# Attention steps: queries and keys transposed by VectorE blocks and a DRAM round trip instead of TensorE, with each step's order written out by hand

## Chip, cores and metric

The kernel runs on one core of a Trainium2 chip. The metric is device microseconds of one launch. The kernel before took 1660.21 us, the median of three runs (1654.62 to 1660.83). Everything is float32.

## The reference

Four layers are added one after the other to x, eight sequences (batches) of 128 tokens by 512. Each layer is a conditioning block followed by a feed-forward block with low-rank experts. The change touches the conditioning block of the third layer (L2), which is an attention with a paged cache of keys and values:

```python
q = _rope(_rmsnorm(q, q_norm_w), pos); k = _rope(_rmsnorm(k, k_norm_w), pos)
kc = k_cache[block_table].reshape(bsz, L, HK, D)
k_all = jnp.concatenate([kc, k], axis=1); v_all = jnp.concatenate([vc, v], axis=1)
scores = jnp.einsum('bqhd,bkhd->bhqk', q, k_all) * SCALE
scores = jnp.where(valid[:, None, None, :], scores, -1e+30)
o = jnp.einsum('bhqk,bkhd->bqhd', jax.nn.softmax(scores, axis=-1), v_all)
return jnp.einsum('bse,de->bsd', o.reshape(bsz, seqlen, HQ * D), Wo)
```

There are 32 query heads and 8 key heads of 128 elements, so four query heads share a key head. Each batch has 512 cached keys, on 16 pages of 32, and 128 new ones. A score is a sum over the 128 head elements, so queries and keys must both lie with the head element on the partitions before the score matmul. Rope and the norm are made with the token on the partitions. Between the two lies a transpose, and that is what the change moves.

## The kernel before, in words

The span has three parts. The first two layers take about the first 320 us. The attention then runs as a loop in `run` (L1176) over 32 steps. The second half of L2 and the fourth layer (`ending`) follow from about 1454 us.

A step n is a pair (qd, p): one key head qd, with its four query heads, and one pair p of batches. For a given step the loop does these things.

- `weigh(n, j)` (L1053), for the pair's batches j = 0 and 1: five score matmuls of 128x512, one for each chunk of 128 keys, into PSUM tiles "st" (three buffers). ScalarE takes the exponential of each into pT.
- `added` (L1067): VectorE adds the five chunks of pT. `divisors` (L1075) sums them over the keys with four small matmuls, takes the reciprocal on VectorE, makes four copies of 32 partitions, and spreads them with three DMAs on SP into R.
- `mix(n, j)` (L1095): five matmuls with the values, accumulated in PSUM tile "av". VectorE multiplies the result by R.
- `project(n+1)` (L946) makes the next step's queries, key and value with `seven` (L908), a product in seven block products instead of eight. Its products one, six and five go through "mm" tiles, of which there are three. Its outputs c11, c12, c21 and c22 leave PSUM through ScalarE (c11) and VectorE (the other three, L961).
- `leave(n-1)` (L1112) is the same `seven` with the output weights. VectorE adds its four results to y2 (L1122), and GpSimd adds two more terms (L1125 and L1130).
- `rotate(n+1)` (L979) and `normed(n+1)` (L1012): GpSimd multiplies the halves of queries and key by the sine table (L990, tiles vq and vk); VectorE multiplies by the cosine table (L994), adds the two (L1018), and multiplies by the reciprocal root of the mean square (L1022), which ScalarE and one VectorE reciprocal prepare.
- `turn_cached(n+1)` (L1025) and `turn(n+1)` (L1036): 8 TensorE transposes of the gathered cached keys, two of the new keys and 8 of the queries, each with a matmul against the identity into PSUM. VectorE copies the keys out (L1033, L1042), and ScalarE the queries (L1049).
- `tokens` (L903) makes the four sums and differences of x that `seven` needs, on VectorE.
- `gather(n+1, "v")` and `gather(n+2, "k")` (L876): GpSimd issues eight indirect DMAs for the values of the next step and eight for the keys of the one after (L886). The gathered keys have two buffers, one for each batch of a pair.

[...] The function `kept` (L840) pins an instruction to its place in program order among the pinned ones of its engine. In the loop it covers GpSimd, most of VectorE and ScalarE, and the R transfers on SP. The matmuls, the PSUM evacuations and the weight loads are not pinned; a scheduler at compile time places them. GpSimd's order in a step is therefore fixed: vq and vk of step n+1, the two additions to y2, eight gathers of values, eight gathers of keys. The gathered keys of step n+1 are first read by `turn_cached(n+1)`, near the end of step n, after `mix(n, 0)` (L1206 to L1208).

Of the kernel before, what the change touches and what calls it, by code (L numbers as in the profile page):

```python
# [17 lines left out]
P = 128  # L18
# [29 lines left out]
def forward(ctx: ExitStack, tc: tile.TileContext, a: dict, out: bass.AP):  # L48
# [16 lines left out]
    rp = ctx.enter_context(tc.tile_pool(name="rp", bufs=1))  # L65
# [24 lines left out]
    second = gate_weights(1)  # L90

# [42 lines left out]
    def rows(name, n, where=const):  # L134
# [38 lines left out]
    selp = w0.tile([P, NB * 4, 4], F32, tag="selp", name="selp")  # L173
    dve.tensor_tensor(
        selp,
        table.rearrange("p (c j) -> p c j", j=4),
        block32.unsqueeze(1).to_broadcast([P, NB * 4, 4]),
        ALU.mult,
    )
    page = const.tile([P, NB * 4], F32, tag="page", name="page")  # L180
    dve.tensor_reduce(page, selp, AX.X, ALU.add)
    dve.tensor_scalar(page, page, 32.0, p_mod32, ALU.mult, ALU.add)
    kvrow = const.tile([P, NQ, NB * 4], I32, tag="kvrow", name="kvrow")
    for qd in range(NQ):
        dve.tensor_scalar(kvrow[:, qd, :], page, float(NQ), float(qd), ALU.mult, ALU.add)
# [472 lines left out]
    with psa:  # L658
# [11 lines left out]
        att = attention(tc, a, x, ident, lens, kvrow, part, ww, wop, ypool, sums, rot, ps_, c2, chunks, mm)  # L670
# [81 lines left out]
    with tc.If(redo > 0):  # L752
        sp.dma_start(x, kept)
        y2 = attention_any(tc, a, x, ident, lens, kvrow, part, ww, wop, ypool, rot, rows, chunks, mm)
# [23 lines left out]
def attention(tc, a, x, ident, lens, kvrow, part, ww, wop, ypool, sums, rot, psa, c2, chunks, mm):  # L778
# [12 lines left out]
    trig, straight, crossed, eps = rot  # L791
# [41 lines left out]
    S = {n: {} for n in range(len(steps))}  # L833
    W, WO = {}, {}
# [41 lines left out]
    def gather(n, what):  # L876
        qd, p = steps[n]
        t = []
        for j in range(2):
# [4 lines left out]
            for c in range(4):  # L884
                i = (2 * p + j) * 4 + c
                kept(pool.indirect_dma_start(  # L886
                    out=d[:, c, :], out_offset=None, in_=kc if what == "k" else vc,
                    in_offset=bass.IndirectOffsetOnAxis(ap=kvrow[:, qd, i : i + 1], axis=0),
                ))
# [12 lines left out]

    def tokens(n):  # L903
        b = 2 * steps[n][1]
        parts = [x[:, 2 * h : 2 * h + 2, (b + j) * P : (b + j + 1) * P] for j in range(2) for h in range(2)]
        S[n]["A"] = combine(wk.tile([P, 4, 2, P], F32, tag="xs", name=f"xs_{n}", bufs=1), *parts)

    def seven(A, B, name, u, two, out2, out4, c11, c12, c21, c22, between=lambda: None):  # L908
# [6 lines left out]

        def into(o, l, r, start):
            for c in range(2):
                pe.matmul(  # L918
                    o, l[:, c, :], r[:, c, :], start=start and c == 0, stop=c == 1, skip_group_check=True
                )  # L920
# [5 lines left out]
        act.copy(u[:, 0], one)  # L926
        into(p6, s2, t2, True)
        into(p5, s1, t1, fresh)
        dve.tensor_tensor(u[:, 1], p6, u[:, 0], ALU.add)
        dve.tensor_tensor(u[:, 2], p5, u[:, 1], ALU.add)  # L930
        into(six, s3, t3, True)
        c22(six, u[:, 2])
        between()
        into(one, a12, b21, False)
        c11(one)
        into(p5, s4, b22, False)
        c12(p5, u[:, 1])
        into(six, a22, t4, False)
# [7 lines left out]
    def project(n):  # L946
# [11 lines left out]
        def put(j, i):  # L958
            def f(ps, u):
                for to, at in places(j, i):  # L960
                    dve.tensor_tensor(to, ps[:, at], u[:, at], ALU.add)  # L961
            return f

        def copied(ps):
            for to, at in places(0, 0):
                act.copy(to, ps[:, at])  # L966

        def two():
# [6 lines left out]
            copied, put(0, 1), put(1, 0), put(1, 1),  # L975
        )
        S[n].update(q=q, k=k)

    def rotate(n):  # L979

        ssq = wk.tile([P, 2, REP + 1], F32, tag="ssq", name=f"ssq_{n}")

        def crossed_terms(m, t, nh):
# [3 lines left out]
            r = wk.tile(full, F32, tag="r" + m, name=f"r{m}_{n}", bufs=1)  # L987
# [9 lines left out]
        def squares(m, t, nh, at):  # L997
            for j in range(2):
                for i in range(nh):
# [988 lines left out]
```

## Time and profile before

| what | value |
|---|---|
| runs of the kernel before, median (lowest to highest) | 1660.21 us (1654.62 to 1660.83) |
| the profiled execution's own time | 1623.05 us |
| its span, first to last instruction | 1621.3 us |
| TensorE / VectorE / ScalarE / GpSimd busy | 1592.8 / 1066.4 / 564.5 / 825.6 us |
| from 457 to 1310 us (24 steps): TensorE / VectorE / ScalarE / GpSimd | 851.55 / 651.36 / 379.85 / 565.41 of 853.0 us |
| from 1454 us to the end: TensorE busy | 154.90 of 167.0 us |
| DMA over the span | 94.41 MB, mean 58 GB/s |
| DMA in the first 41 us | busy share 0.89, 301 GB/s |
| granted TensorE clock, mean | 0.994 |

PE is TensorE's matmuls, PEld its weight loads, DVE is VectorE, ACT ScalarE, POOL GpSimd and SP SyncE; an ending q means the engine's own queue of instructions that are not counted as busy. A profile line names the source line, the engine, the operation, output<-inputs, the shape and the count. A float32 matmul shows as two records. Matmuls overlap, so the pace of TensorE is read from the distance between starts, not from the duration of one record. Issuing a gather is an instruction on POOL (DMA_INDIRECT); its data land later.

### The profile page before, as it was taken

Reading aid. Unit: us, or ns where it says so; the run is one execution under the profiler, and the core shown is the slowest. Engines: PE = TensorE matmul, PEld = TensorE weight load, DVE = VectorE, ACT = ScalarE, POOL = GpSimd, SP = SyncE. Lnnn points to the kernel's source line nnn. Section 1 sums busy time; section 2 is a strip of 40 time slices with the busy share of each in tenths; the row PEclk is TensorE's granted clock in tenths of the full one; section 3 lists DMA queues with packets and bytes.
Section 4 is the critical chain, followed back from the end, with each engine's and each line's share of the span. In section 5 each row is a group of like instructions: output and inputs, shape, how many; then the busy total and the mean of one; then the engine's idle time right before and its main releaser. Section 6 shows DMA issues by size and latency. Waiting matters only on the chain.

```text
span 1621.3 us, 19398 instructions
## 1 busy us (share of the span) xinstructions
PE 1592.8 (98%) x6561; PEld 985.8 (61%) x6561; DVE 1066.4 (66%) x2224; ACT 564.5 (35%) x1390; POOL 825.6 (51%) x778
## 2 busy tenths in 40 slices
PE   9999999999999999999999999999999999999998
PEld 7878885445555555555555556555555655568653
DVE  4575524676878777687877868787786778753141
ACT  1111110254543444455344445544444554420210
POOL 2241106456666666666666656666665676710000
PEclk9999999999999999999999999999999999999899
DMA  8110002221111212112121212212121221311000
GB/s 304 34 39 24 1 1 72 73 61 56 56 64 43 85 43 73 52 61 64 41 87 41 74 48 66 62 43 85 43 73 46 68 62 40 95 49 47 0 18 37
DMA packets 69194, 94.41 MB, mean 58 GB/s; under 512 B 16800, under 2 KB 40544, under 8 KB 68960
## 3 DMA queue, kind: packets, MB, share of 16 engines
q1 hardware_dynamic: 50944, 56.09, 10.9%
q0 software_dynamic: 17056, 36.49, 7.7%
q8 instruction: 54, 0.88, 0.2%
q10 hardware_dynamic: 1088, 0.52, 0.1%
q14 instruction: 52, 0.43, 0.1%
HBM read 76.14 MB, written 4.33 MB: 50 GB/s over the span
## 4 chain that ended last, share of the span: by engine, by line
PE 87%; DVE 8%; issue 3%; POOL 2%; ACT 0%; DMA 0%; SPq 0%; ACTq 0%; DVEq 0%; POOLq 0%
PE av L53 15%; PE st L53 14%; PE q_six L918 7%; PE g L356 7%; PE q_one L918 5%; PE q_five L918 5%; PE wo_two L918 5%; PE dn L356 4%; PE wo_one L918 3%; PE wo_six L918 3%; PE eo_l L53 2%; PE z L53 2%; PE h L1557 2%; PE o L53 2%; DVE q_s L858 2%
## 5 line engine op out<-in xcount | busy, mean ns | idle before, releaser
L886 POOL DMA_INDIRECT kn<-in_k_cache,kvrow x256 | 276.5, 1080 | 80.2 <-issue 66.0
L886 POOL DMA_INDIRECT vals<-in_v_cache,kvrow x256 | 270.0, 1055 | 73.3 <-issue 38.9
L53 PE MATMUL av<-pT,vals 128*128 128x512 f32 x640 | 303.6, 597 | 0.0
L53 PE MATMUL st<-qT,kT 128*128 128x512 f32 x640 | 291.7, 593 | 0.0
L53 PEld LDWEIGHTS av<-pT,vals 128*128 128x128 f32 x640 | 116.5, 190 | 128.9 <-issue 128.9
L53 PEld LDWEIGHTS st<-qT,kT 128*128 128x128 f32 x640 | 116.7, 190 | 124.6 <-issue 96.9
L1061 ACT ACTIVATE pT<-st,hide 128x512 f32<-128x512 f32 x256 | 169.3, 686 | 37.5 <-PE st L53 34.7
L990 POOL TENSOR_TENSOR vq<-q,txq 128x512 f32<-128x512 f32 x64 | 83.5, 1326 | 152.8 <-DVE q L961 152.8
L1072 DVE TENSOR_TENSOR part<-pT 128x512 f32<-128x512 f32 x128 | 85.2, 689 | 64.7 <-ACT pT L1061 64.6
L1049 ACT COPY qT<-qTp 128x512 f32<-128x512 f32 x64 | 37.5, 586 | 206.2 <-PE qTp L1047 206.2
L1130 POOL TENSOR_TENSOR y<-y,uo 128x512 f32<-128x512 f32 x32 | 44.1, 1379 | 112.9 <-DVE y L1122 112.9
L918 PE MATMUL q_one<-q,x 128*128 128x384 f32 x256 | 96.2, 498 | 0.0
L918 PE MATMUL q_six<-q_s,xs 128*128 128x384 f32 x256 | 95.7, 492 | 0.0
L1001 ACT ACTIVATE sqq<-q 128x128 f32<-128x128 f32 x256 | 79.4, 310 | 8.3 <-DVE q L961 1.5
L918 PEld LDWEIGHTS q_six<-q_s,xs 128*128 128x128 f32 x256 | 49.1, 192 | 36.7 <-issue 4.8
L1018 DVE TENSOR_TENSOR rq<-rq,vq 128x1024 f32<-128x1024 f32 x32 | 70.3, 2198 | 1.2 <-POOL vq L990 1.2
L918 PE MATMUL wo_one<-o,oT 128*128 128x256 f32 x256 | 65.8, 379 | 0.0
L918 PEld LDWEIGHTS q_one<-q,x 128*128 128x128 f32 x256 | 46.0, 189 | 31.4 <-issue 6.0
L966 ACT COPY q<-q_one 128x256 f32<-128x256 f32 x32 | 11.9, 372 | 148.2 <-PE q_one L918 138.7
L1087 DVE RECIPROCAL r<-sum 128x128 f32<-128x128 f32 x64 | 60.7, 949 | 0.9 <-PE sum L1081 0.6
L1089 DVE COPY R<-r 32x128 f32<-32x128 f32 x256 | 58.9, 230 | 3.6
L918 PE MATMUL wo_two<-o_s,os 128*128 128x256 f32 x256 | 60.5, 379 | 0.0
(387 smaller groups left out, 2846.0 us busy)
## 6 DMA issues: line engine op xcount, KB each, us to landing
R<-R SPq DMA_DIRECT2D x192, 64.0 KB
q<-in_WqT SPq DMA_DIRECT2D x8, 1024.0 KB
o<-in_WoT SPq DMA_DIRECT2D x8, 1024.0 KB
kn<-in_k_cache,kvrow POOLq DMA_INDIRECT x256, 2.7
vals<-in_v_cache,kvrow POOLq DMA_INDIRECT x256, 2.6
wd<-in_WdT SPq DMA_DIRECT2D x2, 1280.0 KB
wg<-in_WgT SPq DMA_DIRECT2D x9, 256.0 KB
wu<-in_WuT SPq DMA_DIRECT2D x9, 256.0 KB
```

The source lines that it names most:

```text
L53: pe.matmul(o, lhsT, rhs, start=start, stop=stop)
L356: pe.matmul(o, lhsT, rhs, start=start, stop=stop, skip_group_check=True)
L886: kept(pool.indirect_dma_start(out=d[:, c, :], out_offset=None, in_=kc if what == "k" else vc, in_offset=bass.IndirectOffsetOnAxis(ap=kvro ...
L918: pe.matmul(o, l[:, c, :], r[:, c, :], start=start and c == 0, stop=c == 1, skip_group_check=True)
L990: kept(pool.tensor_tensor(u[:, :, :, lo : lo + 64], t[:, :, :, hi : hi + 64], wx[:, :, lo : lo + 64].unsqueeze(2).to_broadcast(part_), ALU ...
L1001: kept(act.activation(sq, t[:, j, i, :], AF.Square, accum_out=ssq[:, j, at + i : at + i + 1]))
L1018: kept(dve.tensor_tensor(r, r, u, ALU.add))
L1061: act.activation(pT[:, c, :, :].rearrange("p i t -> p (i t)"), ps, AF.Exp, bias=hide[:, b, c : c + 1] if c < 4 else 0.0,)
L1072: kept(dve.tensor_tensor(o, l, r, ALU.add))
L1087: kept(dve.reciprocal(r, ps))
L1089: kept(dve.tensor_copy(R[0:32, i * P : (i + 1) * P], r[32 * i : 32 * i + 32, :]))
L1130: kept(pool.tensor_tensor(t, t, u.unsqueeze(1).to_broadcast([P, 2, HW]), ALU.add))
```

## The change

Eighteen TensorE transposes a step go. In their place VectorE transposes blocks of 32x32, and two transfers through DRAM put the blocks in place: four writes on SP, one for each group of 32 partitions, and then a read back (one for the cached keys; one for the queries and two for the new keys). The pages of a gathered key tile are permuted (`kvrow["k"]`), so that the blocks come out in the order of the values.

- `turn_cached(n+1)` moves from the end of step n into the middle of `project(n+1)`, behind its c22.
- `turn(n+1)` moves into `leave(n-1)`, behind its c22, and its transposed queries have one buffer. The read into it waits until `weigh(n, 1)` has read the old ones.
- `rotate(n+1)` moves from the middle of `leave(n-1)` to its beginning.
- The new key is no longer multiplied by its reciprocal root; the factor goes into the scale of the fifth exponential.
- All matmuls, evacuations and transfers of a step are pinned. `mix(n, 0)` runs among and after the scores of `weigh(n, 1)`, `mix(n, 1)` closes step n, and the sums over the keys move into `project` behind its second product.
- The sums of `tokens` are kept from the first use on for the heads 1 to 6.

The diff, cut to its core:

```diff
+    kvrow = {}
+    for what, order in (("v", "p (b c j) -> p b c j"), ("k", "p (b j c) -> p b c j")):
+        selp = w0.tile([P, NB, 4, 4], F32, tag="selp", name="selp_" + what)
+        dve.tensor_tensor(
+            selp,
+            table.rearrange(order, b=NB, c=4),
+            block32.unsqueeze(1).unsqueeze(1).to_broadcast([P, NB, 4, 4]),
+            ALU.mult,
+        )
+        page = const.tile([P, NB * 4], F32, tag="page", name="page_" + what)
...
+    turned, turned_new = (
+        nc.dram_tensor("turned_" + name, (len(steps), 4, 32, 4, m, 32), F32, kind="Internal").ap()
+        for name, m in (("cached", 8), ("new", 2 * REP + 2))
+    )
...
+    kept_sums = {}
+
     def tokens(n):
-        b = 2 * steps[n][1]
+
+
+        qd, p = steps[n]
+        b = 2 * p
+        if 0 < qd < NQ - 1 and p in kept_sums:
+            S[n]["A"] = kept_sums[p]
+            return
         parts = [x[:, 2 * h : 2 * h + 2, (b + j) * P : (b + j + 1) * P] for j in range(2) for h in range(2)]
-        S[n]["A"] = combine(wk.tile([P, 4, 2, P], F32, tag="xs", name=f"xs_{n}", bufs=1), *parts)
-
-    def seven(A, B, name, u, two, out2, out4, c11, c12, c21, c22, between=lambda: None):
+        if 0 < qd < NQ - 1:
+            if not kept_sums:
+                late.append(late[0].tile([P, NP, 4, 2, P], F32, tag="yT", name="xs_all"))
+            S[n]["A"] = kept_sums[p] = combine(late[1][:, p], *parts)
+        else:
+            S[n]["A"] = combine(wk.tile([P, 4, 2, P], F32, tag="xs", name=f"xs_{n}", bufs=1), *parts)
...
+        def now(where):
+            if where in at:
+                at[where]()
...
-        act.copy(u[:, 0], one)
+        kept(act.copy(u[:, 0], one))
+        now("one")
         into(p6, s2, t2, True)
+        now("six")
         into(p5, s1, t1, fresh)
-        dve.tensor_tensor(u[:, 1], p6, u[:, 0], ALU.add)
-        dve.tensor_tensor(u[:, 2], p5, u[:, 1], ALU.add)
+        kept(dve.tensor_tensor(u[:, 1], p6, u[:, 0], ALU.add))
+        now("u1")
+        kept(dve.tensor_tensor(u[:, 2], p5, u[:, 1], ALU.add))
+        now("u2")
         into(six, s3, t3, True)
         c22(six, u[:, 2])
-        between()
+        now("c22")
         into(one, a12, b21, False)
         c11(one)
+        now("c11")
         into(p5, s4, b22, False)
         c12(p5, u[:, 1])
+        now("c12")
...
+        both = wk.tile([P, 2 * REP + 2, HD], F32, tag="r", name=f"r_{n}", bufs=1)
+        views = {"q": both[:, 0 : 2 * REP], "k": both[:, 2 * REP :]}
...
+    def rotated(n):
+        for m in "qk":
+            r, u = S[n]["r" + m]
+            kept(dve.tensor_tensor(r, r, u, ALU.add))
+
+    def roots(n):
+        s = S[n]
+        s["rs"] = rs = wk.tile([P, 2, REP + 1], F32, tag="rs", name=f"rs_{n}")
+        kept(act.activation(rs, s["ssq"], AF.Sqrt, bias=eps, scale=1.0 / HD))
 
     def normed(n):
+
         s = S[n]
-        s["rest"]()
-        rs = wk.tile([P, 2, REP + 1], F32, tag="rs", name=f"rs_{n}")
-        kept(act.activation(rs, s["ssq"], AF.Sqrt, bias=eps, scale=1.0 / HD))
-        for r, u in (s["rk"], s["rq"]):
-            kept(dve.tensor_tensor(r, r, u, ALU.add))
+        r, rs = s["rq"][0], s["rs"]
         kept(dve.reciprocal(rs, rs))
-        for m, at, nh in (("k", REP, 1), ("q", 0, REP)):
-            r = s["r" + m][0]
-            dve.tensor_tensor(r, r, rs[:, :, at : at + nh].unsqueeze(3).to_broadcast([P, 2, nh, HD]), ALU.mult)
-            s[m] = r
+        kept(dve.tensor_tensor(r, r, rs[:, :, 0:REP].unsqueeze(3).to_broadcast([P, 2, REP, HD]), ALU.mult))
...
     def turn_cached(n):
 
         s = S[n]
-        kT = wk.tile([P, 2, LK], F32, tag="kT", name=f"kT_{n}")
+        t = wk.tile([P, 4, 8, 32], F32, tag="kt", name=f"kt_{n}", bufs=1)
         for j in range(2):
-            ps = psa.tile([P, 512], F32, tag="mm", name=f"kTc_{n}_{j}", bufs=3)
-            for c in range(4):
-                pe.transpose(ps[:, c * P : (c + 1) * P], s["kc"][j][:, c, :], ident)
-            dve.tensor_copy(kT[:, j, 0:L], ps)
-        s["kT"] = kT
+            kept(dve.transpose(
+                t[:, :, 4 * j : 4 * j + 4, :], s["kc"][j].rearrange("p c (b d) -> p b c d", b=4)
+            ))
+        s["kT"] = wk.tile([P, 4, 8, 32], F32, tag="kT", name=f"kT_{n}")
+        written(turned[n], t)
+        kept(sp.dma_start(s["kT"], turned[n].rearrange("b i a m d -> (b i) a m d")))
+
+    def written(dst, t):
+        for q in range(4):
+            kept(sp.dma_start(dst[:, :, q].rearrange("b i m d -> i b m d"), t[32 * q : 32 * q + 32]))
 
     def turn(n):
 
         s = S[n]
-        ps = psa.tile([P, 2, P], F32, tag="mm", name=f"kTn_{n}", bufs=3)
+        m = 2 * REP
+        t = wk.tile([P, 4, m + 2, 32], F32, tag="kt", name=f"qkt_{n}", bufs=1)
+        kept(dve.transpose(t, s["both"].rearrange("p m (b d) -> p b m d", b=4)))
+        s["qT"] = wk.tile([P, 4, m, 32], F32, tag="qT", name=f"qT_{n}", bufs=1)
+        s["kn"] = wk.tile([P, 2, 4, 32], F32, tag="kTn", name=f"kTn_{n}", bufs=1)
+        written(turned_new[n], t)
+        src = turned_new[n].rearrange("b i a m d -> (b i) a m d")
+        kept(sp.dma_start(s["qT"], src[:, :, 0:m, :]))
         for j in range(2):
-            pe.transpose(ps[:, j, :], s["k"][:, j, 0, :], ident)
-        dve.tensor_copy(s["kT"][:, :, L:LK], ps)
-        qT = []
-        for j in range(2):
-            ps = psa.tile([P, 512], F32, tag="mm", name=f"qTp_{n}_{j}", bufs=3)
-            for i in range(REP):
-                pe.transpose(ps[:, i * P : (i + 1) * P], s["q"][:, j, i, :], ident)
-            t = wk.tile([P, REP * P], F32, tag="qT", name=f"qT_{n}_{j}", bufs=3)
-            act.copy(t, ps)
-            qT.append(t)
-        s["qT"] = qT
-
-    def weigh(n, j):
+            kept(sp.dma_start(s["kn"][:, j], src[:, :, m + j, :]))
...
+            kept(pe.matmul(
+                ps, s["kT"][:, c, 4 * j : 4 * j + 4, :] if c < 4 else s["kn"][:, j],
+                s["qT"][:, :, REP * j : REP * (j + 1), :].rearrange("p a i t -> p i a t"), start=True, stop=True,
+            ))
+            kept(act.activation(
                 pT[:, c, :, :].rearrange("p i t -> p (i t)"), ps, AF.Exp,
-                bias=hide[:, b, c : c + 1] if c < 4 else 0.0,
-            )
-        return pT
-
-    def added(n, j, pT):
+                **(
+                    dict(bias=hide[:, b, c : c + 1]) if c < 4
+                    else dict(bias=0.0, scale=s["rs"][:, j, REP : REP + 1])
+                ),
+            ))
+            for f in then.get(c, ()):
+                f()
...
+        S[n]["sum", j] = ps = psa.tile([P, P], F32, tag="st", name=f"sum_{n}_{j}", bufs=3)
...
     def first(n):
         tokens(n)
         project(n)
+        if n == 0:
+            turn_cached(n)
+        for j in range(2):
+            squares(n, "q", j, range(REP))
+            squares(n, "k", j, range(1))
         rotate(n)
+        roots(n)
+        rotated(n)
         normed(n)
+        turn(n)
 
     def run(pool_, end, bank):
         late.append(pool_)
...
         for n, (qd, p) in enumerate(steps):
+
             after = n + 1 if 0 < n < len(steps) - 1 else None
-            pT = weigh(n, 0)
-            added(n, 0, pT)
-            if last:
-                mix(n - 1, 1, last)
-            divisors(n, 0)
-            if last:
+            sums_of, turned_next = added(n, 0), lambda: n + 1 < len(steps) and turn_cached(n + 1)
+            weigh(n, 0)
+            if n:
+                divided(n - 1, 1)
+            for _ in sums_of:
+                pass
+            if n:
                 outputs(n - 1)
             if after:
-                project(after)
-                leave(n - 1, lambda: rotate(after))
-            elif last:
-                leave(n - 1)
+                project(after, {
+                    "six": lambda: summed(n, 0), "u1": lambda: inverted(n, 0), "u2": lambda: spread(n, 0),
+                    "c22": turned_next, "c11": lambda: (squares(after, "k", 0, (0,)), squares(after, "q", 0, (0, 1))),
+                    "c12": lambda: squares(after, "q", 0, (2, 3)),
+                })
+                rotate(after)
+                leave(n - 1, {
+                    "one": lambda: (
+                        squares(after, "q", 1, range(REP)), squares(after, "k", 1, (0,)), roots(after),
+                    ),
+                    "c22": lambda: (rotated(after), normed(after), turn(after)),
+                })
+            else:
+                summed(n, 0)
+                inverted(n, 0)
+                spread(n, 0)
+                turned_next()
+                if n:
+                    leave(n - 1)
             if after:
                 if n + 2 == len(steps):
                     end.load_w2()
                     end.load_aw()
                     end.shifted()
-                normed(after)
                 gather(after, "v")
-                if n + 2 < len(steps):
-                    if steps[n + 2][1] == 0:
-                        weights(steps[n + 2][0])
-                    else:
-                        tokens(n + 2)
-            if last and p == 0:
+                if n + 2 < len(steps) and steps[n + 2][1] == 0:
+                    weights(steps[n + 2][0])
+            if n and p == 0:
                 out_weights(qd)
-            last = weigh(n, 1)
-            added(n, 1, last)
-            mix(n, 0, pT)
-            if n + 1 < len(steps):
-                turn_cached(n + 1)
-            divisors(n, 1)
-            if n + 1 < len(steps):
-                turn(n + 1)
+            mixed = mix(n, 0)
+            some = lambda: next(mixed)
+            weigh(n, 1, {2: (some,), 3: (some,), 4: (some, some, some)})
+            for _ in added(n, 1):
+                pass
+            divided(n, 0)
+            summed(n, 1)
+            inverted(n, 1)
+            spread(n, 1)
+            for _ in mix(n, 1):
+                pass
             if n + 2 < len(steps):
                 gather(n + 2, "k")
-                if steps[n + 2][1] == 0 and n:
-                    W[steps[n + 2][0]].factors()
+                if n:
+                    if steps[n + 2][1] == 0:
+                        W[steps[n + 2][0]].factors()
                     tokens(n + 2)
             if n and p == 0:
...
-    yT = early.tile([P, DC, NT], F32, tag="yT", name="y2T")
+    Y2T = []
...
```

`squares`, `inverted`, `spread`, `mix` and `divided` hold the former bodies of `rotate`, `divisors` and `mix`, cut into pieces so that they can be placed singly. `eps` and the rotary pool move to other pools.

## The prediction

> **What bounds the kernel now.** I read the page's busy times first, then the order of time of one steady step (492.75 to 528.25 us) on TensorE, GpSimd and VectorE, then the waits of GpSimd.
>
> ```profile
> PE 1592.8 (98%) x6561; PEld 985.8 (61%) x6561; DVE 1066.4 (66%) x2224; ACT 564.5 (35%) x1390; POOL 825.6 (51%) x778
> ...
> 492.75 4.46 PE L53 MATMUL st<-qT,kT 128*128 128x512 f32 x10
> ...
> 523.83 1.04 PE L1032 MATMUL kTc<-ident,kn 128*128 128x128 f32 x8
> 524.80 0.43 PE L1081 MATMUL sum<-part,ones 128*32 128x128 f32 x8
> ...
> 526.12 0.38 PE L1041 MATMUL kTn<-ident,rk 128*128 128x128 f32 x2
> 526.47 0.65 PE L1047 MATMUL qTp<-ident,rq 128*128 128x128 f32 x4
> 526.96 1.02 PE L53 MATMUL av<-pT,vals 128*128 128x512 f32 x2
> 527.82 0.60 PE L1047 MATMUL qTp<-ident,rq 128*128 128x128 f32 x4
> 528.25 1.02 PE L53 MATMUL st<-qT,kT 128*128 128x512 f32 x2
> ```
>
> TensorE has no gaps: ten score records take 4.3 us from start to start, and nothing else in the step is stretched. It is the bound. A step takes 35.50 us from score to score. From starts, the transposes take 0.97 (kTc), 0.35 (kTn), 0.49 and 0.43 (qTp), 2.24 us in all. A step without them is 33.26 us of TensorE.
>
> The second view is GpSimd's order of time, from this step into the next.
>
> ```profile
> 510.00 2.51 POOL L990 TENSOR_TENSOR vq<-q,txq 128x512 f32<-128x512 f32 x2 [4.70 <-DVE q L961]
> 512.47 0.87 POOL L990 TENSOR_TENSOR vk<-k,txk 128x128 f32<-128x128 f32 x2
> 515.96 1.38 POOL L1130 TENSOR_TENSOR y<-y,uo 128x512 f32<-128x512 f32 x1 [2.62 <-DVE y L1122]
> 517.29 1.71 POOL L1125 TENSOR_TENSOR y<-uo,y 128x256 f32<-128x256 f32 x1
> 519.15 0.99 POOL L886 DMA_INDIRECT vals<-in_v_cache,kvrow  x1 [0.15 <-issue]
> ...
> 529.94 0.94 POOL L886 DMA_INDIRECT kn<-in_k_cache,kvrow  x1 [0.30 <-issue]
> ...
> 539.93 0.94 POOL L886 DMA_INDIRECT kn<-in_k_cache,kvrow  x1 [0.30 <-issue]
> ```
>
> GpSimd idles 4.70 and 2.62 us a step, and for the rest it works. The last key gather of the step starts at 539.93, which is 11.7 us into the next step (from 528.25). Today nobody needs it before that step's end. VectorE's order of time shows what GpSimd waits for, and what stands in its way:
>
> ```profile
> 509.41 0.42 DVE L961 TENSOR_TENSOR q<-q_six,uq 128x256 f32<-128x256 f32 x1 [0.67 <-PE q_six L918]
> ...
> 513.20 1.22 DVE L994 TENSOR_TENSOR rq<-q,tsq 128x1024 f32<-128x1024 f32 x1
> ...
> 516.12 2.29 DVE L1018 TENSOR_TENSOR rq<-rq,vq 128x1024 f32<-128x1024 f32 x1
> ...
> 525.13 1.28 DVE L1033 COPY kT<-kTc 128x512 f32<-128x512 f32 x2
> ```
>
> [...]
> - [...] the 1024-element addition at 516.12 takes 2.29 us where the product of the same size takes 1.22. GpSimd's first y addition ends at 517.34, and 517.34 + 1.2 is where it ends (518.41). GpSimd's second, of 256 elements, waits for that in turn (1.71 us).
> - [...] The trace has one such instruction (L107, 32 elements, 204 ns)[...]. My estimates are 0.65 and 1.45 us where the next follows at once. The large shapes are not in the trace.
> - [...] SP's longest waits stand at R's transfers (628.5 us for VectorE's copies).
> - [...] The records here are 272 to 277 ns, but starts are 0.12 apart. The distance decides what removal is worth.
>
> **Part by part.** *TensorE's 18 transposes*: minus 2.24 us a step. The score matmuls now read queries in runs of 32 elements. No row shows that; I take nothing, and say below what covers it.
>
> *Copies*: minus two of 0.62 us (from starts) and one of 0.36 on VectorE, the key's product of 0.71, and two of 0.58 on ScalarE. Added on VectorE: 2x0.65 + 1.45. VectorE gains nothing or loses some 0.4 us a step. The kept token sums take 4x0.34 us off it in 20 of the steps.
>
> *SP*: twelve transfers a step more, at 0.4 to 0.6 us of issue (as R's and the weights'). They move 2x512 + 2x640 KB, some 60 GB/s beside the mean of 58; the first stage moved 301. The read of the queries waits for the last score of batch 1, because the tile has one buffer. Behind it on SP stand the keys' reads, the weight loads and R's transfers for batch 1. The queries are needed 3x0.86 + 0.35 + 5x0.86 = 7.2 us after that score. I price the read at 0.5 issue + 2.7 landing (as a gather's) + 512 KB at 301 GB/s, 4.9 us: covered. Without that cover it would cost its excess each step. The head's weights (1.5 MB, some 8 us after that score) make VectorE wait for about 2.5 us seven times; its wait for keys, below, hides that, otherwise it is 17 us.
>
> *Pinning, and the sums*: sums wait for four additions that end about 2.2 us after the last score; the two products ahead take 2.58. In steps 0 and 31 nothing lies between, some 2.3 us each; that cancels with the 36 transposes gone at the start (4.5 us).
>
> *turn_cached moved*, the step that decides. Its VectorE transposes now stand behind c22 of `project(n+1)`, some 11.5 us into the step, and wait for keys whose last gather is only issued at 11.7 and lands 2.7 us later (median of the gathers). Queued behind on VectorE are c12 and c21, the rotation, the norm, the new transposes and `leave`'s evacuations. TensorE waits for c12 (its second product of `leave` needs that "mm" buffer), and GpSimd for c21. GpSimd's additions to y follow `leave`'s c21, the gathers follow these, and the next transposes follow the gathers. That is a ring of one turn a step:
>
> - two additions to y: 519.15 - 515.96 = 3.19
> - first value gather to last key gather: 539.93 - 519.15 = 20.78 seen; 15x1.25 = 18.75 if all stand as close as the closest; I take the middle, 19.8, as VectorE now stands idle beside some of them
> - landing: 2.7
> - second key transpose: 0.65
> - c12's two additions, c21's first, and the step to GpSimd: 0.34 + 0.28 + 0.42 + 0.17 = 1.21
> - from GpSimd's vq to VectorE's addition of it: the two vq (2x1.25) and VectorE's two products (1.15 + 0.35) now ask at the same time and exclude each other, 4.0; then three evacuations of `leave`, 1.15: 5.15. If they didn't exclude each other, 2.9
> - addition (1.15), key's addition (0.35), reciprocal (0.2), product (1.15): 2.85
> - new transpose: 1.45
> - c11, c12, c21 of `leave`, and the step to GpSimd: 1.2
>
> Sum 38.2 us. TensorE's 33.3 fits inside with 4.9 us to spare, so the 2.24 us saved turn into waiting. That slack also covers the strided reads, the queries' round trip and SP's order. A step before takes 35.6 on the mean (386.29 to 1383.96 is 28 steps). The ring closes 29 times (steps 2 to 30): 29x(38.2 - 35.6) = +75 us. Nothing else moves by more than its cover: span 1621 + 75 = 1696, own time 1698. The median of the runs is 37 us above the profiled execution. I add the 75 to it: 1735. Were that offset a slower TensorE, steps in which TensorE waits would lose less of it, up to 24 us.
>
> **The rivals.**
> *A, faster: the keys land in time.* Against it speaks 11.7 + 2.7 on today's clock. For it: gathers at 18.75, landing at 2.4 (the least seen) and no exclusion (2.9) close the ring in 34.6. It decides from a ring of 35.6 downward. Then 29x(34.6 - 35.6) = -29: 1631. With the ring below 33.3 TensorE binds again, 29x2.3 = 67 less: 1593.
> *B, VectorE's transposes at half the rate.* The ring gets 0.55 + 1.35 longer, and with gathers at 20.78, 41.1: +159, 1819. Nothing in the trace excludes it[...].
> *C, the round trip of the queries comes last,* with the keys early. It decides above 7.2 us; at 10 us a step takes 33.3 + 2.8 = 36.1: +15, 1675. The 301 GB/s speaks against it.
> *D, nothing measurable:* the ring ends near 35.6, the saving goes into one wait: 1660.
>
> **How the numbers follow.** Forecast 0.60, B 0.15, C 0.07, A 0.13, D 0.05. About 0.5% (8 us) is what a measurement of this kernel can tell from no change; so slower 0.82, same 0.05, faster 0.13. Forecast's own range: gathers from 18.75 to 20.78 and half the exclusion give 36 to 39.2, 1672 to 1765. To hold 8 in 10 it must take in B, C and D: 1655 to 1820. A is left out.
>
> **What would show it.** Right: an idle time of 4 to 6 us before VectorE's second key transpose, put down to the gathers' landing; TensorE idle before `leave`'s second product, released by VectorE's c12; GpSimd's gathers back to back into its vq; a period near 38; transposes of 0.7 and 1.5 us; the cosine product at about 2 us instead of 1.22. Wrong: no idle time at the key transposes and a period near 33; or scores that wait for the read of the queries.

## The result and the profile after

The kernel after takes 1759.71 us (1747.56 to 1763.68, 4 runs), the kernel before on the same chip 1660.52 us (1654.62 to 1666.6, 4 runs): ratio 1.0585 [1.0519, 1.0651], +99 us where +75 was forecast. The profiled execution of after took 1762.12 us (span 1759.9).

The page's busy times of after:

```profile
PE 1600.0 (91%) x5985; PEld 942.3 (54%) x5985; DVE 1106.2 (63%) x2123; ACT 536.5 (30%) x1324; POOL 858.6 (49%) x778
```

TensorE lost its share: 98% before, 91% now, with 576 instructions fewer and yet 7 us more busy time. So it waits, and part of its work runs slower. The page's groups (busy, mean ns of one; idle before, and what ended it) name the waits:

```profile
L1099 PE MATMUL st<-qT,kT 128*128 128x512 f32 x512 | 274.8, 676 | 69.4 <-DMA qT<-turned_new 63.3
...
L946 PE MATMUL wo_one<-o,oT 128*128 128x256 f32 x256 | 71.1, 402 | 27.0 <-ACT k L1000 25.0
...
L1066 DVE STREAM_TRANSPOSE kt<-kn 128x512 f32<-128x512 f32 x64 | 43.2, 695 | 42.0 <-DMA kn<-in_k_cache,kvrow_k 42.0
...
L946 PE MATMUL wo_two<-o_s,os 128*128 128x256 f32 x256 | 64.9, 399 | 1.2 <-DVE vals L995 1.2
```

The third line is the wait that the prediction named: VectorE's key transposes stand 42 us for the gathers. It hardly reaches TensorE here: the last line is the product of `leave` that the prediction had waiting for c12, and it waits 1.2 us in all. The first is the one it had ruled out: scores wait 63 us for the read of the queries. The second is new; it comes back below. TensorE's order of time, one step and the beginning of the next:

```profile
642.20 3.60 PE L1099 MATMUL st<-qT,kT 128*128 128x512 f32 x8
645.63 1.02 PE L1099 MATMUL st<-qT,kTn 128*128 128x512 f32 x2
...
659.80 1.13 PE L946 MATMUL wo_one<-o,oT 128*128 128x256 f32 x4 [2.82 <-ACT k L1000]
...
675.32 4.56 PE L1150 MATMUL av<-pT,vals 128*128 128x512 f32 x10
684.30 6.16 PE L1099 MATMUL st<-qT,kT 128*128 128x512 f32 x8 [4.42 <-DMA qT<-turned_new]
690.29 1.02 PE L1099 MATMUL st<-qT,kTn 128*128 128x512 f32 x2
691.15 1.13 PE L946 MATMUL q_one<-q,x 128*128 128x384 f32 x3
```

The step from 642.20 is 42.10 us long, the one from 684.30 only 36.46, and so on in turn. The ten score records at 642.20 take 4.29 us to the next start (646.49), as before; those at 684.30 take 6.85 (691.15 - 684.30). Why they do, the windows show (length, PE busy, PEld, DVE, ACT, POOL, granted clock, DMA share, GB/s):

```profile
680.00:682.00 2.00, 0.00 (x0) 0.00 (x0) 0.79 (x2) 0.00 (x0) 1.39 (x3) 1.00 0.56 128
682.00:684.00 2.00, 0.00 (x0) 0.00 (x0) 0.08 (x1) 0.00 (x0) 1.70 (x2) 0.61 1.16 317
684.00:686.00 2.00, 1.70 (x2) 0.84 (x3) 0.00 (x0) 0.00 (x0) 1.39 (x3) 0.50 0.28 68
686.00:688.00 2.00, 2.00 (x4) 0.80 (x3) 0.00 (x0) 0.69 (x1) 1.60 (x2) 0.50 0.20 66
688.00:690.00 2.00, 2.00 (x5) 0.88 (x4) 0.69 (x1) 1.05 (x2) 1.49 (x2) 0.68 0.17 53
```

TensorE's granted clock falls to half during the idle time, some 2.6 us after its last record ended (679.88), and stays there 6.8 us: a mean of 0.61 from 682 to 684 is a drop at 682.4, and 0.68 from 688 to 690 a return at 689.3. This stall of 4.4 us so costs 4.4 + 2.6 (6.85 - 4.29). SP's order of time shows why the read of the queries is late in one step and not in the other:

```profile
632.24 1.86 SPq L1075 DMA_DIRECT2D turned_new<-qkt  x4
636.52 0.59 SPq L1087 DMA_DIRECT2D qT<-turned_new  x1
637.16 1.29 SPq L1089 DMA_DIRECT2D kTn<-turned_new  x2
640.04 2.05 SPq L1142 DMA_DIRECT2D R<-R  x3
...
665.41 0.39 SPq L885 DMA_DIRECT2D o<-in_WoT  x1
...
669.76 2.22 SPq L1075 DMA_DIRECT2D turned_new<-qkt  x4
677.56 1.78 SPq L1142 DMA_DIRECT2D R<-R  x3
679.57 0.58 SPq L1087 DMA_DIRECT2D qT<-turned_new  x1
```

In the first step the read is issued 4.28 us after the first write. In the second, R's three transfers stand ahead of it. They wait for VectorE's copies (676.45 to 677.5), and the read leaves 9.81 us after the first write. It is needed at 679.88 and usable 4.73 us after its issue. R comes first in every second step, which are those in which SP also issues a weight load (pairs 0 and 2). The program asks for the read first, and pins these transfers in that order; it is the compiled order that has the read behind. Why the pins did not hold it there is open.

### The profile page after: what moved, and what is told of

The parts are those of the page before. It is cut to its first block, busy times and chain, and to the rows that moved or that the text cites. A ratio compares the mean times of both kernels' runs of the same rounds, so it can differ in the third digit from the quotient of the medians.

```text
span 1759.9 us, 18914 instructions
## 1 busy us (share of the span) xinstructions
PE 1600.0 (91%) x5985; PEld 942.3 (54%) x5985; DVE 1106.2 (63%) x2123; ACT 536.5 (30%) x1324; POOL 858.6 (49%) x778
## 4 chain that ended last, share of the span: by engine, by line
PE 57%; DVE 13%; POOL 6%; issue 6%; another core or an unknown queue 6%; DMA 6%; ACT 4%; SPq 2%; ACTq 0%; DVEq 0%; POOLq 0%
PE st L1099 11%; PE av L1150 8%; PE g L362 6%; DVE part L1119 5%; PE q_six L946 4%; PE dn L362 4%; PE q_five L946 3%; DMA qT<-turned_new 3%; PE q_one L946 2%; PE eo_l L53 2%; POOL vk L1033 2%; PE wo_one L946 2%; DVE qkt L1082 2%; PE wo_two L946 2%
## 5 line engine op out<-in xcount | busy, mean ns | idle before, releaser
L1099 PE MATMUL st<-qT,kT 128*128 128x512 f32 x512 | 274.8, 676 | 69.4 <-DMA qT<-turned_new 63.3
L897 POOL DMA_INDIRECT kn<-in_k_cache,kvrow_k x256 | 264.0, 1031 | 81.8 <-issue 77.6
L897 POOL DMA_INDIRECT vals<-in_v_cache,kvrow_v x256 | 267.4, 1044 | 73.2 <-issue 58.8
L1033 POOL TENSOR_TENSOR vq<-q,txq 128x512 f32<-128x512 f32 x64 | 118.4, 1869 | 199.3 <-DVE q L995 177.5
L1119 DVE TENSOR_TENSOR part<-pT 128x512 f32<-128x512 f32 x128 | 113.2, 886 | 128.2 <-ACT pT L1103 110.7
L1160 DVE TENSOR_TENSOR oT<-av,R 128x512 f32<-128x512 f32 x64 | 44.2, 691 | 93.4 <-DMA R<-R 70.2
L1134 DVE RECIPROCAL rr<-sum 128x128 f32<-128x128 f32 x64 | 60.9, 952 | 37.4 <-PE q_five L946 15.3
L946 PEld LDWEIGHTS wo_one<-o,oT 128*128 128x128 f32 x256 | 50.0, 200 | 46.1 <-ACT k L1000 31.8
L946 PE MATMUL q_six<-q_s,xs_all 128*128 128x384 f32 x192 | 69.8, 486 | 0.0
L1066 DVE STREAM_TRANSPOSE kt<-kn 128x512 f32<-128x512 f32 x64 | 43.2, 695 | 42.0 <-DMA kn<-in_k_cache,kvrow_k 42.0
L1140 DVE COPY R<-rr 32x128 f32<-32x128 f32 x256 | 63.3, 247 | 3.7
```

The costliest lines, as they stand in the source:

```text
L897: kept(pool.indirect_dma_start(out=d[:, c, :], out_offset=None, in_=kc if what == "k" else vc, in_offset=bass.IndirectOffsetOnAxis(ap=kvro ...
L946: kept(pe.matmul(o, l[:, c, :], r[:, c, :], start=start and c == 0, stop=c == 1, skip_group_check=True))
L1033: kept(pool.tensor_tensor(u[:, :, :, lo : lo + 64], t[:, :, :, hi : hi + 64], wx[:, :, lo : lo + 64].unsqueeze(2).to_broadcast(part_), ALU ...
L1099: kept(pe.matmul(ps, s["kT"][:, c, 4 * j : 4 * j + 4, :] if c < 4 else s["kn"][:, j], s["qT"][:, :, REP * j : REP * (j + 1), :].rearrange( ...
L1119: kept(dve.tensor_tensor(o, l, r, ALU.add))
L1134: kept(dve.reciprocal(r, S[n]["sum", j]))
```

## The experiments

The occasions differ: the kernel before took 1660.5 us with the result, 1693.8 and 1692.4 with e1 to e7, and 1620.8 and 1621.4 with e8 to e12. So each ratio is against the kernel before on the same occasion. The chip alone is not what differs: e5 to e12 all ran on one chip (e1 to e4 on another), where the kernel before took 1692.4 us and, later, 1620.8. The last two values agree with the profiled execution of before (1623). Theory 1: the ring of the prediction sets the step. Theory 2: the read of the queries, late by SP's order, does. Theory 3 came with the first four runs.

**e1: the keys' gathers ahead of the values'.** This opens the ring.

```diff
+                if n + 2 < len(steps):
+                    gather(n + 2, "k")
                 gather(after, "v")
...
-                gather(n + 2, "k")
+                if not after:
+                    gather(n + 2, "k")
```

> The eight key gathers of step n+2 are issued ahead of the eight value gathers of step n+1, so the keys land some 10 us earlier and the ring over the gathers is open. Kernel after: 1759.7 us, steps of 39.2 us on the mean, in pairs of 42 and 37. Theory 1, the ring is the whole cost and the scores' waits for the queries only follow from a late VectorE: both waits go, a step takes 33.5 to 34.5 us, time 1595 to 1625. Theory 2, in every second step (the steps with a weight load) the queries' read is queued on SP behind the three R transfers, which wait for VectorE's copies near the step's end: the wait for the queries (4.4 us idle and some 2.9 us of half-clock scores after it) stays in those steps whatever the keys do; a pair takes 2x33.6 + 7.3 = 74.5, time about 1760 - 15x(79.1 - 74.5) = 1690, at most 1710. No wait for kn under either.

1796.65 us, ratio 1.0591 [1.0538, 1.0645]. No theory gave that. The waits for gathered keys are gone and those for the queries remain (the page puts 64.3 us on them), but steps are 43 to 48 and 35 to 37 us in turn. TensorE now idles up to 7 us before q_five of `project` (the page puts 55.2 us on that), where nothing that the change touched is late.

**e2: R's transfers on ScalarE's queue.** This frees the read of the queries.

```diff
-            kept(sp.dma_start(R[32 * i : 32 * i + 32, :], R[0:32, :]))
-        kept(sp.dma_start(sums[2 * n + j : 2 * n + j + 1, :], R[0:1, :]))
+            kept(act.dma_start(R[32 * i : 32 * i + 32, :], R[0:32, :]))
+        kept(act.dma_start(sums[2 * n + j : 2 * n + j + 1, :], R[0:1, :]))
```

> Only the R transfers and the row of sums move from SP's queue to ScalarE's; the gathers stay as in the kernel after. Theory 1 (ring): the wait of VectorE for kn is now there in every step, the ring turns once in 37.5 us (from one addition to y to the next, 633.26 to 670.79 in the kernel after), time about 1760 - 30x(39.2 - 37.6) = 1710. Theory 2 (queue order): the scores' waits for the queries go, and if the ring is no bound of its own a pair takes 79.1 - 7.3 = 71.8, time about 1650. ScalarE may wait for R's copies ahead of its exponentials; it has 7.8 us of idle time there.

1797.98 us, ratio 1.0598 [1.0545, 1.065]. The page's score group:

```profile
L1099 PE MATMUL st<-qT,kT 128*128 128x512 f32 x512 | 241.0, 604 | 11.8 <-DMA qT<-turned_new 5.2
```

The wait of 69 us is down to 11.8 and the mean record to 604 ns, so the cause of that wait, and of the half clock, is shown. Yet no time is gained: steps are now 40.8 us on the mean, nearly all between 39 and 42.

**e3: both edits. e4: both, and the queries' tile in two halves with three buffers** (two for the new keys), so that a read need not wait for the old scores.

```diff
+        s["qT"] = [wk.tile([P, 4, REP, 32], F32, tag="qT", name=f"qT_{n}_{j}", bufs=3) for j in range(2)]
...
+        for j in range(2):
+            kept(sp.dma_start(s["qT"][j], src[:, :, REP * j : REP * (j + 1), :]))
```

> Both edits together. Theories 1 and 2 together: neither kn nor the queries are waited for, the step is TensorE's own 33.3 to 34.5 us, time 1760 - 30x(39.2 - 34) = 1604, between 1590 and 1625: faster than the kernel before by 2 to 4%. If a third thing holds TensorE (late signals to ScalarE's c11 copy, DRAM traffic, a lower clock), a step stays above 36 us and the time above 1660.

> As the one with both edits, and the transposed queries in two tiles with three buffers, the new keys in two, so that the read waits for its writes alone and not for the last scores of batch 1. If that wait is covered once R is off SP's queue, the same time as with both edits within 8 us. If the read comes just in time there (in the kernel after it lands some 1 us ahead of the scores in the undisturbed steps), some 5 to 25 us less.

1772.23 us, 1.0455 [1.0393, 1.0516], and 1769.1 us, 1.0413 [1.0357, 1.0468]: alike, so the single buffer of the queries costs nothing that shows on this occasion. Both waits are gone, and most steps still take 37 to 43 us, with idle times before q_five and q_six of up to 6.8. Three of e3's steps (11, 15 and 19 of the loop) take 34.3 to 34.4 and have hardly any idle time. What differs in them is when TensorE's completion is seen. Two lines of TensorE and ScalarE in the result's own trace of after:

```profile
652.21 1.45 PE L946 MATMUL q_one<-q,x 128*128 128x384 f32 x4
...
659.21 0.37 ACT L1000 COPY q<-q_one 128x256 f32<-128x256 f32 x1 [10.69 <-remote]
```

ScalarE's copy needs that product and nothing else that is late. The product's last record ends at 653.66; the copy starts 5.5 us later ("remote": the trace names no source on this core for the signal that ended the wait). In the profile of before on which the prediction rests no such delay was over 0.2 us. Theory 3: some of TensorE's signals arrive late, on some occasions, by up to 7.1 us (e1), and what is built on them waits. The lateness is not spread at random: in the trace of after, from 370 to 1300 us, this copy is 4.7 to 5.8 us late in every second step, those that begin without a stall of TensorE, and at most 0.1 us in the others.

**e5: the kernel before, unchanged,** with a profile taken on such an occasion.

> The kernel before, unchanged, as a control: on this chip its runs are 1693.8 us, 33 us above the runs first shown and 72 above the profiled execution first shown. In the kernel after and in the four experiments TensorE's signals of finished products reached VectorE and ScalarE 2 to 8 us late in the middle of most steps (in the kernel before's first profile never over 0.1 us). Theory 3a, the lateness belongs to the new transfers: none here, steps of 35.5 us, and the profiled time near the first one. Theory 3b, it belongs to the chip or the run: some steps here wait as well (a project of 14 us instead of 9), and they make the 30 to 70 us.

1693.87 us beside 1692.42, ratio 0.9997 [0.9977, 1.0017]. ScalarE's group of the copy behind `project`'s second product, by the trace's groups, first in the profile of before that the prediction used, then in e5:

```profile
L926 ACT COPY uq<-q_one 128x384 f32<-128x384 f32 x32 | 15.3, 479 | 123.4 <-PE q_one L918 123.4
```

```profile
L926 ACT COPY uq<-q_one 128x384 f32<-128x384 f32 x32 | 15.3, 478 | 189.0 <-PE q_six L918 97.9 <-PE q_five L918 49.2 <-remote 16.1
```

The same copy waits 65.6 us longer, 2 us a step, and the kernel is 72 us slower than on the undisturbed occasion (1693 - 1621). So the late signals are not of the change's making.

**e6: e1 without both trips through DRAM** (the scores read the blocks as VectorE left them). **e7: e1 without the cached keys' trip alone.**

```diff
+        t = s["kT"] = wk.tile([P, 4, 8, 32], F32, tag="kT", name=f"kT_{n}")
...
-        s["kT"] = wk.tile([P, 4, 8, 32], F32, tag="kT", name=f"kT_{n}")
-        written(turned[n], t)
-        kept(sp.dma_start(s["kT"], turned[n].rearrange("b i a m d -> (b i) a m d")))
```

The cut shows the keys' part; e6 leaves out the queries' four writes and three reads in the same way.

> Keys first, as in e1, and both trips through DRAM are left out: the scores read the blocks as VectorE's transposes left them (so the scores are of the wrong keys; the fifth chunk reads queries' blocks). Every engine does the same work; 20 transfers of a step and some 90,000 packets of the launch go. Theory 3a (the late signals come with the transfers): no late signals, no waits, steps of 33.3 to 34.3 us, 6.5 us less than e1's 40.7: about 1797 - 30x6.6 = 1600, faster than before by 4 to 6%. Theory 3b or a cause in the new order itself (sums in the middle of project, waits of several engines on TensorE): late signals stay, steps over 37 us, time over 1680.

> As e1, keys first, with the cached keys' trip alone left out (the scores are of the wrong keys); queries and new keys still go through DRAM. The five transfers that are left out are 1 MB of the 2.3 MB and about a third of the packets. If lateness grows with the transfers, something between e1 and e6, 1650 to 1750. If it hangs on the queries' trip (whose packets are the small ones, 1024 of 128 bytes a step for the new keys), as e1 within 20 us.

e6: 1721.49 us, 1.0148 [1.0092, 1.0204]. e7: 1785.44 us, 1.0544 [1.0494, 1.0595]. Beside e1's 1.0591, the keys' trip is hidden and the queries' is not. e6 still has steps of 38 us on the mean, and of 33.6 to 34.4 where no signal is late, which is in every fourth step: the late signals don't need the trips.

**e8: before, e9: after, e10: e6, each without the gathers of steps 2 to 31** (these steps reuse step 1's keys and values).

```diff
     def gather(n, what):
+        if n > 1:
+            S[n][what + "c"] = S[1][what + "c"]
+            return
```

> The kernel before, with the gathers of steps 2 to 31 left out (those steps use the keys and values of the first two). Its usual runs take 1693 us here and its steps 37.4 us, its first profiled execution 1623 and 35.5, and the difference is signals of TensorE that reach VectorE and ScalarE late while GpSimd issues gathers. Theory 3c, the gathers make the signals late: no late signals, steps of 35.5 us, 1615 to 1630 us, 4% under the kernel before. If lateness has another source (profile, chip, DRAM): 1670 to 1695.

> The kernel after with the same gathers left out; trips through DRAM, order of SP and everything else stay. Theory 3c: no late signals and no ring, so what is left is the queries' read behind R in every second step: a pair takes 2x33.4 + 7.3 = 74, 37.0 a step against 35.5 in the kernel before without gathers, time 1623 + 30x1.5 = 1668, against about 1790 of the kernel after on this chip. If the ring alone had made the change slow (theory 1): steps of 33.4 us, 1560. If the trips make signals late: over 1720.

> Trips and gathers both left out: the new order and VectorE's transposes alone. Theory 3c: TensorE has no wait left, 33.3 to 33.8 us a step, about 1623 - 30x1.9 = 1566, within 10 us. That would be what the change could have given. Over 1600: the new order itself has waits that I haven't seen.

This occasion had no late signals, so it could not test whether gathers cause them; that stays open. It gave clean prices instead. e8: 1621.01 us, 1.0001 [0.9992, 1.001]: gathers cost the kernel before nothing. e9: 1668.66 us, 1.0291 [1.0274, 1.0308], as theory 2 expected (1668). With no ring, steps average 36.8 us, and in every second one the scores wait 3.1 to 4.3 us for the queries and then take 6 to 7.4 us instead of 4.29. Its page:

```profile
L1102 PE MATMUL st<-qT,kT 128*128 128x512 f32 x512 | 272.3, 671 | 60.6 <-DMA qT<-turned_new 55.8
```

e10: 1583.27 us, 0.9779 [0.9761, 0.9797]: steps of 33.6 us without a gap. That is 17 us more than expected, part of it in the last three steps (39.4, 34.4 and 42.7 us).

**e11: after, unchanged, and e12: the kernel of e3,** on the undisturbed occasion.

> The kernel after, unchanged, once more, for a session in which TensorE's signals come in time (the kernel before then takes 1621 us; with late signals 1660 to 1694, and this kernel some 1760 to 1790). Without late signals: the kernel without gathers took 1668.7 us, steps of 36.8 us. The ring over the gathers turned once in 37.5 us in the first profile. If the ring binds (the prediction), steps are 37.5 to 38.5 us and the time 1690 to 1720, with waits for kn; if the gathers cost nothing once signals are in time, 1669 us, as without them.

> Keys first and R on ScalarE's queue, once more. Without late signals: no wait for kn, none for the queries, steps of 33.6 to 34.4 us (its undisturbed steps took 34.35 us in the first run), time 1583 (the order without trips and gathers) to 1610, faster than the kernel before at 1621 by 1 to 2%. With late signals: 1765 to 1780 again, 4.5% slower.

e11: 1739.79 us (1729.59 to 1742.11), ratio 1.071 [1.0665, 1.0755], +118 us; 20 to 50 us above what was expected. e12: 1603.04 us (1598.74 to 1608.07), 0.9891 [0.9854, 0.9928], in the range expected. e12's page:

```profile
PE 1539.5 (96%) x5985; PEld 929.1 (58%) x5985; DVE 1113.3 (70%) x2123; ACT 533.3 (33%) x1324; POOL 853.5 (53%) x778
...
L1099 PE MATMUL st<-qT,kT 128*128 128x512 f32 x512 | 241.4, 605 | 11.7 <-DMA qT<-turned_new 6.0
```

Its steps take 33.56 us, every fourth 34.36:

```profile
608.15 3.60 PE L1099 MATMUL st<-qT,kT 128*128 128x512 f32 x8
...
641.72 3.60 PE L1099 MATMUL st<-qT,kT 128*128 128x512 f32 x8
```

With gathers and trips in place, these two edits take 137 us off the kernel after and make it 1.1% faster than before. That holds while signals are timely; with late ones the same kernel was 4.5% slower (e3).

e11 shows the ring without disturbance. GpSimd's order of time, from one addition to y to the next step's:

```profile
633.96 1.65 POOL L1187 TENSOR_TENSOR y<-y,uo 128x512 f32<-128x512 f32 x1 [4.44 <-DVE y L1179]
635.57 1.17 POOL L1182 TENSOR_TENSOR y<-uo,y 128x256 f32<-128x256 f32 x1
636.89 1.26 POOL L897 DMA_INDIRECT vals<-in_v_cache,kvrow_v  x1
...
657.03 0.94 POOL L897 DMA_INDIRECT kn<-in_k_cache,kvrow_k  x1 [0.30 <-issue]
661.54 3.70 POOL L1033 TENSOR_TENSOR vq<-q,txq 128x512 f32<-128x512 f32 x2 [3.56 <-DVE q L995]
...
671.49 1.65 POOL L1187 TENSOR_TENSOR y<-y,uo 128x512 f32<-128x512 f32 x1 [4.44 <-DVE y L1179]
```

The last gather leaves at 657.03, and GpSimd's next work waits 3.56 us for VectorE, whose order of time in e11, with the one line of TensorE that waits for it, is:

```profile
659.82 0.71 DVE L1066 STREAM_TRANSPOSE kt<-kn 128x512 f32<-128x512 f32 x1 [4.14 <-DMA kn<-in_k_cache,kvrow_k]
660.46 0.38 DVE L995 TENSOR_TENSOR q<-q_five,uq 128x256 f32<-128x256 f32 x1
660.76 0.27 DVE L995 TENSOR_TENSOR vals<-q_five,uq 128x128 f32<-128x128 f32 x1
...
661.18 1.97 PE L946 MATMUL wo_two<-o_s,os 128*128 128x256 f32 x8 [3.39 <-DVE vals L995]
...
661.49 1.21 DVE L1037 TENSOR_TENSOR r<-q,tsq 128x1024 f32<-128x1024 f32 x1
...
662.62 1.50 DVE L1037 TENSOR_TENSOR r<-k,tsk 128x256 f32<-128x256 f32 x1
...
665.27 1.47 DVE L1047 TENSOR_TENSOR r<-r,vq 128x1024 f32<-128x1024 f32 x1
...
668.93 1.51 DVE L1082 STREAM_TRANSPOSE qkt<-r 128x1280 f32<-128x1280 f32 x1
```

VectorE stands 4.14 us before the second key transpose for the gathered keys; behind it stands c12 (660.46, 660.76), and TensorE's second product of `leave` waits 3.39 us for c12. Over the whole execution this wait is 47.4 us, and in most steps more follows it than in the one shown. An earlier step of e11, after e11's page:

```profile
L946 PE MATMUL wo_two<-o_s,os 128*128 128x256 f32 x256 | 72.3, 433 | 47.4 <-DVE vals L995 47.4
...
424.94 3.75 PE L946 MATMUL wo_two<-o_s,os 128*128 128x256 f32 x8 [3.28 <-DVE vals L995]
428.48 1.91 PE L946 MATMUL wo_six<-o_s,os 128*128 128x256 f32 x4
```

The eight records take 3.54 us to the next start; in the step at 661.18 they take 1.81 (662.99), and without a stall 1.72. TensorE's granted clock is 0.50 from 425 to 429. Of the 14 such stalls between 380 and 1480 us, of 3.1 to 3.4 us each, nine are followed by 2.2 to 3.6 us for these records and five by 1.8.

## Why the prediction was right, and where it wasn't

The sign and the size held: slower, by 99 us where 75 were forecast. The place held for VectorE and, without late signals, for TensorE (47.4 us for c12 in e11). In the result's own trace TensorE waits only 1.2 us for c12; its waits there are for the late copy, one product earlier (25.0 us), and for the read of the queries (63.3 us). Opening the ring on such an occasion gained nothing (e1, 1.0591 beside 1.0585). So it is in part luck that the result came near the forecast. Term by term, against the turn of the ring in e11:

| term | forecast | e11 |
|---|---|---|
| additions to y | 3.19 | 2.93 (633.96 to 636.89) |
| first to last gather | 19.8 | 20.14 (to 657.03) |
| landing | 2.7 | 2.79 (to 659.82) |
| second key transpose | 0.65 | 0.64 (to 660.46) |
| c12, c21, step to GpSimd | 1.21 | 1.08 (to 661.54) |
| vq until VectorE adds it | 5.15 | 3.73 (to 665.27) |
| addition to product | 2.85 | 3.66 (to 668.93) |
| new transpose | 1.45 | 1.44 (to 670.37) |
| three puts, step to GpSimd | 1.2 | 1.12 (to 671.49) |
| sum | 38.2 | 37.53 |

- **VectorE and GpSimd at the same time.** Instructions grew, but not those that were expected: in e11 the cosine product kept its 1.21 us (2 were expected), and GpSimd's vq pair took 3.70 where the two took 2.51 before; VectorE's key product took 1.50 (0.41 before, at 514.34), and its addition 1.47 (1.15 expected). That the two engines exclude each other, behind the forecast's 4.0 us, was the author's estimate: these longer times are shown, what makes them longer is not. The mis-sized term is the 5.15: the evacuations ran beside vq. Part of it came back in the next row. For the addition at 516.12 the prediction's sum is 0.13 us off: 517.34 + 1.2 is 518.54, not 518.41.
- **TensorE's saving, the strided reads, the transposes.** A step without gaps takes 33.56 us (33.26 forecast), ten scores 4.29 as before, VectorE's transposes 0.70 and 1.51, or 0.64 and 1.44 to the next start. The forecast's 0.65 and 1.45, and the low chance of rival B, were the author's estimates: the one block transpose in the trace of before has 32 elements a partition (204 ns) and does not show them. The measured times agree with the forecast, and rival B is out. Sums behind two products: no idle time before them in e12. The wait of 0.95 us in every fourth step stands before the other sums, those of batch 1.
- **The step that failed** is "That slack also covers the strided reads, the queries' round trip and SP's order". The price of the read was right: 4.9 us forecast, 4.61 from its issue (680.28) to the scores in e11. The cover was right too. The point of issue was not: the part on SP put R's transfers *behind* the read, while in every second step they stand ahead of it, and R waits for VectorE's copies near the step's end. The read so left about 5.5 us later than the writes allowed. Rival C was given 0.07 as an alternative to the ring. It isn't an alternative: both hold, in the same step, one after the other. Scores that wait for the read of the queries were one of the prediction's own signs of being wrong, and they came.
- **How they add up.** In e11 two steps, from 642.89 to 721.18, take 78.29 us. Twice 33.56 is 67.12; the wait for c12 adds 3.39, that for the queries 4.31, the half clock behind that 7.03 - 4.29 = 2.74; 0.73 remains. The ring so closes in every second step, not in each: the stall for the queries stretches the other turn to some 41 us, and there the keys are early. The forecast had TensorE wait 2 x 4.9 = 9.8 us in two steps, and it loses 11.2. That total came out near, but in this pair only about a third of it is from the cause named. Over all pairs, with the half clock that mostly follows the wait for c12, it is nearer half, as the removals show. Steps average 39.31 us from 370.09 to 1510.10 (29 steps), 29 x (39.31 - 35.6) = 108 of the 118 us.
- **Shown by removal.** On one chip: after 1739.8; without gathers, so without the ring, 1668.7 (-71); without the trips as well 1583.3 (-85). The trips as such are a small part of the 85: e12 has them and takes 1603. So the read of the queries, where the compiled order has it, makes the kernel slower than 1621 even without the ring. The ring alone was not run while signals were timely; an estimate from 37.53 us a turn is 29 x (37.53 - 35.6) = +56.
- **The 37 us between profile and runs.** The prediction carried them over. By e5 and the trace of after they were late signals, which the profiled execution of before happened not to have; a slower run of before from that occasion has no trace. With the result before took 39 us more than undisturbed (1660.5 against 1621.4) and after 20 (1759.7 against 1739.8), so 118 shrank to 99. That the waits overlap fits the 1.2 us for c12. The text's "steps in which TensorE waits lose less of it, up to 24" had this with another cause. The kernel of e3 loses far more to them: 169 us (1772.2 - 1603.0, e12), where before lost 72 (1693.8 - 1621.4). That its pinned order lets one late evacuation hold up all behind it is argued, not shown.
- **Open:** what makes TensorE's signals late on some occasions, and then in some steps and not in others; why the compiled order swapped the transfers; and why the last steps of e12 take 42.2, 34.4 and 42.7 us.

## What to carry to other kernels

When a step is moved, go round the ring that it joins, each engine's queue and the DMA queues too, in the order in which the *compiled* program issues them: here, in every step with a weight load, two transfers stood the other way round than in the source, and a covered read became as large a loss as the ring. Two waits in one step can both be real, since the second begins where the first left off; undo each by itself and then both. If the profiled time and the median of the runs differ by more than their scatter, find what differs before a number is carried from one to the other.

## What the hardware showed beyond that

- Stalls of TensorE of 4.3 to 4.4 us, in after and e11, were followed by half clock (for 6.8 us in after), so that ten scores took 6.85 and 7.03 us instead of 4.29. In e9 stalls of 3.1 to 3.4 us were followed by it too, at 589.09 for 3.4 us (granted clock 0.55 from 589 to 591, 0.60 from 591 to 593, 1.00 around them), and ten scores took 6.0 to 6.1 us. Of e11's stalls of that length nine of 14 brought it and five did not. So the length of a stall alone did not decide.
- The 512 KB read of the queries from DRAM was usable 4.73 us (after) and 4.61 us (e11) after its issue. Where nothing stood between, it was issued 4.28 us after the first of the four writes ahead of it (after, at 636.52).
- TensorE's signals reached ScalarE and VectorE up to 7.1 us late (e1) in some steps of some occasions, and never by more than 0.2 us in the undisturbed traces of before, e11 and e12. On the occasions with late signals the kernel before took 2.4 to 4.5% longer (1660.5 and 1693.8 against 1621.4).
